# A Mamba stage in slots: the softplus logarithm in open PSUM sums, one activation table set for exp and log, seven of 32 state products per chunk on GpSimd, and VectorE's remaining product issued last in its slot

## The chip, the cores and the metric

The kernel runs on one core of one Trainium2 chip. The metric is device time in microseconds (us); a kernel is run several times and the median is compared. Engines are named as in the profile: PE is TensorE (PEld its weight loads), DVE is VectorE, ACT is ScalarE, POOL is GpSimd, SP is SyncE, which here only issues DMAs.

## The reference, cut to what matters

The whole network is a convolution with attention, then a two-direction Mamba layer with a small MLP, then a mixture of experts. The change touches the Mamba layer alone:

```python
dt = softplus(einsum('blr,dr->bld', dt, dt_proj_w) + dt_proj_b)
A = -exp(A_log)
dA = exp(dt[..., None] * A)
dBx = dt[..., None] * Bm[:, :, None, :] * xc[..., None]
def step(h, inp):
    dA_t, dBx_t, C_t = inp
    h = dA_t * h + dBx_t
    y = einsum('bds,bs->bd', h, C_t)
    return (h, y)
...
y = ys + xc * Dp
y = y * silu(z)
```

It is run over 4096 tokens, 512 inner channels and 16 states, once forwards and once backwards. The two results are added to `m`, and then come a layer norm, an MLP with a leaky ReLU, `m + p`, the residual, and a layer norm for the experts.

## The kernel before, in words

Everything is fp32. The Mamba layer is cut into 16 **chunks** of 512 tokens; even chunks are the forward direction, odd ones the backward direction. A chunk is cut into 32 **slots**, `at` = 0 to 31. A slot is (e, k, j): e = at // 8 is one of four tiles of 128 channels, k one of four groups of states, j one of two halves. So a slot is a [128, 2, 512] tile: 1024 elements in each partition. The order of all engines' queues is written out by hand in the loop over `slots` at the end of `mamba_phase`; nothing is reordered.

Each slot n needs, in this order:

- `inflow(n)` on POOL: dbx = dt·x · B, read from two tiles that DMAs have spread over the partitions. Three buffers, `up`.
- `decay(n)` on ACT: two exponentials of 512 elements into a PSUM tile `da`, of which there are two.
- `bring(n)` on ACT, or on POOL in the slots of `LONG`: one column of dbx gets the state that the chunk starts with.
- `recur(n)` on DVE: the scan h = da·h + dbx. Right behind it the product of h with C, into an SBUF tile `h` of which there are four (`hp`). In the slots of `POOLED` (4, 10, 12, 18, 28 before) the scan writes straight into `h`, and POOL makes the product in place (`pooled`), issued a slot later, behind `inflow`.
- `keep(n)` on ACT: a copy of the last column into `state`, issued a slot later, ahead of `decay(n + 2)`.
- `sum_states` on PE: four matmuls that add the states of a pair of slots into `y`, issued two slots after the pair's first, three where that one is pooled.
- `close(i, e)` on DVE, once in eight slots: y times the gate silu(z). Before the change it is issued in slots 0, 8, 16 and 24, behind the product.

In slot n the loop issues `inflow(n + 2)`, `keep(n - 1)`, `decay(n + 1)`, `bring(n + 1)` and `recur(n)`. The other work of the stage is spread among the slots as generators, one step a slot:

- `prepare(q)` makes chunk q's inputs while chunk q-1 is running. It starts in slot 27 of the chunk before that one (`AHEAD` = 5), and takes one step per slot: input projection, causal convolution on PE, SiLU of xc in slot 8, the x_proj matmul in slot 9, dt_proj in slots 11 to 14, then softplus, in the form relu(v) + log(1 + exp(-|v|)) with a rounding correction, the gate's projection z, and the products dt·x (`dt_piece`), which go through DRAM (`dtd`) to be spread over partitions.
- `output(i)` multiplies a finished chunk by the output weights, in slots 1 to 3 of the next one.
- `tail(c)` is the layer norm, MLP, residual and second layer norm for a pair of chunks. Each `yield` names the engine that its next step needs, and the step is taken only in slots that are not in `FULL` for that engine.

PSUM is small: two banks for `mm` (the projections, dt and softplus sums), one `tl` bank for the tail, one `y` bank, two `da` tiles. The SiLU of the gates runs in slot 0 (L2019), the one of xc in the step behind the convolution (L1389). The compiler puts an activation table load ahead of any activation whose function the loaded set lacks.

Of the kernel before, what the change touches and what calls it, by code (L numbers as in the profile page):

```python
# [1255 lines left out]
def mamba_phase(cx, early, w_in, w_x, w_out, w1, w2, x1d, ud, bcd, dtd, x2d, u2d, usum):  # L1256
# [12 lines left out]
    with ExitStack() as ctx:  # L1269
# [59 lines left out]

        def mm_psum():  # L1330
            return pmm.tile([P, N], FP, name="mm", tag="mm")
# [25 lines left out]
        def prepare(q):  # L1357
# [31 lines left out]
            nc.scalar.activation(xc, xc, AF.Silu)  # L1389
            yield  # L1390
            ps = mm_psum()
            nx = DR + 2 * DS
            for e in range(ET):
                nc.tensor.matmul(ps[0:nx, :], wx[d][:, e, :], xc[:, e, :], start=e == 0, stop=e == ET - 1)
            yield
            xd = few()[0:nx, :]
            nc.scalar.copy(xd, ps[0:nx, :])

# [7 lines left out]
            for e in range(ET + 1):  # L1406
                if e > 0:
                    ex = early.wide("ex")[:, :, 0:N] if e == 1 else ex
                    dt = dt or sp.tile([P, ET, N], FP, name="dt", tag="dt")
# [10 lines left out]
            for e in range(ET + 2):  # L1420
                if e < ET:
                    rd = rds[e] = few()
                    nc.scalar.activation(rd, ex[:, e, :], AF.Identity, scale=-1.0, bias=-1.0)
                    nc.scalar.add(rd, rd, 1.0)
                if e > 1:
                    nc.scalar.copy(dt[:, e - 2, :], sums.pop(e - 2))
                if 0 < e <= ET:
                    ps = sums[e - 1] = mm_psum()
                    for v, x in enumerate((rds.pop(e - 1), ex[:, e - 1, :], dt[:, e - 1, :])):
                        nc.tensor.matmul(ps, cx.ident, x, start=v == 0, stop=v == 2)  # L1430
                yield


            nc.scalar.activation(ex, ex, AF.Ln, bias=1.0)
            zs = in_pair(q, ET)
            yield
            got["dt"] = dt
            for at, (v, e) in enumerate(((0, 0), (1, 0), (0, 1), (0, 2), (0, 3), (1, 1))):
                if at == 3 and q > 1:
                    load_first(q, 0)  # L1440
                dt_piece(q, v, e, ex)
                if at in (0, 2):
                    z = sp.tile([P, 2, N], FP, name="z", tag="z", bufs=3)
                    got.setdefault("z", []).append(z)
                if at < 4:
                    nc.scalar.copy(z[:, at % 2, :], zs[at % 2])  # L1446
                if at == 1:
                    zs = in_pair(q, ET + 2)
                    if q + 1 < 2 * NCH:
                        load_u(q + 1)  # L1450
                yield

        def dt_piece(q, v, e, ex=None, eng=nc.gpsimd):
# [3 lines left out]
            if v == 0:  # L1457
                eng.tensor_tensor(dt[:, e, :], dt[:, e, :], ex[:, e, :], ALU.add)
                if q < 2:
                    return  # L1460
                if e == 0:
                    firsts[q] = ip.tile([P, ET], FP, name="first", tag="first", bufs=1)
                nc.gpsimd.tensor_tensor(firsts[q][:, e : e + 1], dt[:, e, 0:1], odd[:, 0:1], ALU.add)
                if e % 2:
                    first_rows[q, e // 2] = cx.rows.tile([P, 2], FP, name="first_row", tag="first_row", bufs=2)
                    nc.sync.dma_start(out=first_rows[q, e // 2], in_=firsts[q][:, e - 1 : e + 1])
# [70 lines left out]
        def tail(c):  # L1537
# [3 lines left out]
            yield from layer_norm(cx, tl, tl_psum, m, hn, nc.gpsimd, 2)  # L1541
            x1 = tl.tile([P, CT, N], FP, name="x1", tag="ln_xc")
            nc.sync.dma_start(out=x1, in_=x1d[c])
            for t in range(CT):
# [3 lines left out]
            yield "DMA"  # L1548
            yield "POOL"
# [34 lines left out]
        def start():  # L1584
# [93 lines left out]
            for z in got["z"]:  # L1678
                nc.scalar.activation(z, z, AF.Silu)
# [293 lines left out]
        with tc.manual_schedule(engines=ORDERED):  # L1973
# [5 lines left out]
            for n, (i, e, k, j) in enumerate(slots):  # L1979
# [40 lines left out]
                if i == 0:  # L2020
                    step(begin)
# [377 lines left out]
```

## Time and profile before

| | |
|---|---|
| median of 3 runs | 4099.89 us (4095.22 to 4108.44) |
| profiled execution, its own time | 4114.01 us |
| its span, first to last instruction | 4112.1 us |
| Mamba slots, first scan to last | 1946.9 to 3818 us of the span |
| time from a chunk's first scan to the next one's, chunks 4 to 14 | 113.5 to 119.2 us, mean 117 |
| one scan, 128x1024 | 2347 ns |
| one product with C on DVE, 128x1024 | 1225 ns |
| the same product on POOL | 2355 ns |
| one decay activation, 128x512 (two in a slot) | 692 ns |
| one ACT table load | 1283 ns |
| from scan to scan: slot with a DVE product / pooled slot | 3.59 us / 2.26 us |

The profile page gives busy time by engine and by line for one execution. Engine idle time has a releaser beside it: the instruction whose end let the engine go on. A fp32 matmul of 512 columns appears as two instructions; their pitch, not the modelled duration, tells how long PE is held: 0.43 us each where the granted clock is 1.0, 0.85 where it is 0.5.

### The profile page before, as it was taken

The numbers are of one execution on the slowest core, as the hardware profiler recorded it, in microseconds if no ns is written. First come the engines' busy times: TensorE is split into PE (matmuls) and PEld (weight loads), VectorE is DVE, ScalarE is ACT, GpSimd is POOL, SyncE is SP. The second block draws the span as 40 slices with busy tenths as digits, with TensorE's granted clock in tenths as the row PEclk, the third lists the DMA queues.
The fourth block names the chain that finished last, engine by engine and source line by source line (L and its number), as shares of the span: only waits on it lengthen the run. The fifth ranks groups of instructions, "written<-read, shape, count | busy, mean of one in ns | idle before, by whom it ended". The sixth has DMA issues, their size and how long they took to land. (4 is left out here: it accounts for less than half of the span.)

```text
span 4112.1 us, 43244 instructions
## 1 busy us (share of the span) xinstructions
PE 3586.2 (87%) x14792; PEld 1183.0 (29%) x14792; DVE 3503.9 (85%) x2919; ACT 2667.8 (65%) x4152; POOL 1836.6 (45%) x1284
## 2 busy tenths in 40 slices
PE   6769888999999999998888788888888888876898
PEld 2324332222222222222222222222223232222444
DVE  8998877989889889877899999999999999999322
ACT  1111226988887878876777777778787777775222
POOL 3020000000000000001888889888888989888100
PEclk9889998999999999998888998898899899888999
DMA  6232215223322223214334344344333434332221
GB/s 208 93 98 95 81 59 157 51 60 65 65 56 62 63 54 65 58 42 122 118 106 129 116 124 130 121 119 129 113 113 119 144 109 133 117 122 90 64 62 55
DMA packets 164324, 399.93 MB, mean 97 GB/s; under 512 B 36997, under 2 KB 46469, under 8 KB 163838
## 3 DMA queue, kind: packets, MB, share of 16 engines
q1 hardware_dynamic: 137166, 304.26, 24.0%
q0 software_dynamic: 24624, 84.43, 8.9%
q10 hardware_dynamic: 2304, 8.39, 0.6%
q8 instruction: 118, 1.93, 0.2%
q14 instruction: 112, 0.92, 0.1%
HBM read 268.17 MB, written 79.56 MB: 85 GB/s over the span
## 5 line engine op out<-in xcount | busy, mean ns | idle before, releaser
L1890 POOL TENSOR_TENSOR dbx<-dtxr,b 128x1024 f32<-128x1024 f32 x512 | 1202.9, 2360 | 201.9 <-DVE da L1903 80.2
L1044 ACT ACTIVATE e<-sc 128x1024 f32<-128x1024 f32 x1024 | 993.8, 1023 | 178.5 <-PE sc L1037 152.7
L1903 DVE TENSOR_TENSOR_SCAN da<-da,state,dbx 128x1024 f32<-128x1024 f32 x432 | 1013.9, 2347 | 16.9 <-ACT da L1880 7.2
L954 DVE TENSOR_TENSOR s<-s,e 128x1024 f32<-128x1024 f32 x768 | 880.5, 1216 | 25.1 <-ACT e L1044 24.4
L1880 ACT ACTIVATE da<-dtr,aneg 128x512 f32<-128x512 f32 x1024 | 708.2, 692 | 33.2 <-DMA dtr<-dtd 3.7
L1037 PE MATMUL sc<-q,kS 32*128 32x512 f32 x4096 | 652.8, 650 | 15.6 <-ACT e L1044 11.4
L961 PE MATMUL av<-e,vT 128*32 128x512 f32 x4096 | 557.2, 612 | 0.4 <-ACT e L1044 0.4
L1908 DVE TENSOR_TENSOR h<-da,c 128x1024 f32<-128x1024 f32 x432 | 529.1, 1225 | 33.2 <-PE y L1943 1.2
L977 POOL DMA_DIRECT2D s<-s x94 | 81.5, 874 | 953.0 <-DVE s L954 901.7
L1943 PE MATMUL y<-h,sel 128*32 128x512 f32 x2048 | 368.9, 654 | 99.2 <-DVE h L1908 74.7
L462 PE MATMUL cv<-v,u 128*128 128x512 f32 x928 | 414.9, 607 | 28.7 <-DVE v L286 13.3
L1037 PEld LDWEIGHTS sc<-q,kS 32*128 32x128 f32 x4096 | 211.5, 185 | 460.0 <-issue 259.4
L1339 PE MATMUL mm<-u,win 128*128 128x512 f32 x464 | 252.8, 695 | 77.1 <-ACT z L1446 25.8
L462 PEld LDWEIGHTS cv<-v,u 128*128 128x128 f32 x928 | 179.4, 195 | 261.9 <-issue 228.4
L560 DVE SCALAR_TENSOR_TENSOR acc<-pad,wdw_s,acc 128x768 f32<-128x768 f32 (+1 forms) x192 | 236.0, 1234 | 19.9 <-ACT acc L553 14.2
L1934 ACT COPY state<-da 128x2 f32<-128x2 f32 x431 | 67.9, 158 | 264.6 <-DVE h L1908 263.5
L1385 PE MATMUL mm<-xp,taps 128*128 128x512 f32 x480 | 212.8, 595 | 0.0
L143 POOL TENSOR_TENSOR ln_few<-ln_few,minus_half 128x4 f32<-128x4 f32 x29 | 34.8, 1201 | 397.5 <-DMA ln_few<-ln_row 259.6
L954 DVE TENSOR_TENSOR s<-e 128x1024 f32<-128x1024 f32 x128 | 151.9, 1217 | 62.2 <-ACT e L1044 53.5
L1903 DVE TENSOR_TENSOR_SCAN h<-da,state,dbx 128x1024 f32<-128x1024 f32 x80 | 187.5, 2344 | 13.0 <-ACT state L1934 11.7
L961 PEld LDWEIGHTS av<-e,vT 128*32 128x32 f32 x4096 | 82.0, 108 | 400.5 <-issue 390.3
L1913 POOL TENSOR_TENSOR h<-h,c 128x1024 f32<-128x1024 f32 x80 | 188.4, 2355 | 1.0 <-ACT state L1934 1.0
(379 smaller groups left out, 3940.9 us busy)
## 6 DMA issues: line engine op xcount, KB each, us to landing
dtr<-dtd SPq DMA_DIRECT2D x128, 512.0 KB
dtxr<-dtd SPq DMA_DIRECT2D x128, 512.0 KB
s<-s POOLq DMA_DIRECT2D x94, 512.0 KB, 5.9
b<-bcd SPq DMA_DIRECT2D x64, 256.0 KB
c<-bcd SPq DMA_DIRECT2D x64, 256.0 KB
dtd<-dt SPq DMA_DIRECT2D x64, 256.0 KB
dtd<-few SPq DMA_DIRECT2D x64, 256.0 KB
u<-uv SPq DMA_DIRECT2D x24, 640.0 KB
```

The lines of the kernel that those rows point to most:

```text
L462: nc.tensor.matmul(rows4(ps), u[:, dy, P * ci : P * ci + P], v[:, dy : dy + HR, ci, :], start=dy + ci == 0, stop=dy == k - 1 and ci == CT - 1,
L560: nc.vector.scalar_tensor_tensor(o, src, w_ap, o, ALU.mult, ALU.add)
L954: nc.vector.tensor_tensor(z, x, y, ALU.add)
L961: nc.tensor.matmul(g.av[32 * h : 32 * h + 32, :], vT[:, kb, P * t + 32 * h : P * t + 32 * h + 32], es[h // 2][:, h % 2, :], start=kb == 0, ...
L1037: nc.tensor.matmul(ps[h // 2][:, h % 2, :], kS[r, t, P * kb : P * kb + P], q_t[r, t, :], start=True, stop=True,)
L1044: nc.scalar.activation(e, ps[i], AF.Exp)
L1339: nc.tensor.matmul(ps, win[d][:, t, P * e : P * e + P], u[:, t, ::-1] if d else u[:, t, :], start=t == 0, stop=t == CT - 1,)
L1880: nc.scalar.activation(da[:, v, :], dts[i, e, j][0][:, v, :], AF.Exp, scale=aneg[i % 2][:, a : a + 1])
L1890: nc.gpsimd.tensor_tensor(u, dts[i, e, j][1], bcs[i, k][0][:, None, :].to_broadcast([P, 2, N]), ALU.mult)
L1903: nc.vector.tensor_tensor_scan(das[n].rearrange("p v n -> p (v n)"), da.rearrange("p v n -> p (v n)"), u.rearrange("p v n -> p (v n)"), st ...
L1908: nc.vector.tensor_tensor(h, da, bcs[i, k][1][:, None, :].to_broadcast([P, 2, N]), ALU.mult)
L1943: nc.tensor.matmul(ys[i, e][32 * j : 32 * j + 32, :], cx.sel, hs[n + j // 2][:, j % 2, :], start=False, stop=k == SQ - 1,)
```

## The change

1. `exp_and_log()` loads a table set that holds both exp and log, right behind each SiLU. Before, exp, log and SiLU were in three sets.
2. In `prepare`, log(1 + exp(-|v|)) is no longer added to dt on POOL. PE's sum of the other terms stays open (`stop=False`), ACT takes the logarithm by tiles of 512 (`logs`), and one more identity matmul adds it and closes the sum; ACT then copies the finished dt out (`keep_dt`). The first column, which the next chunk's start needs, is copied by ACT from PSUM, where POOL made it before.
3. The gate projections (`z_of`, `keep_z`) are spread: the first two beside x_proj (slots 9 to 11), the other two among the softplus steps. The dt·x pieces, four on POOL, are issued in slots 21, 23, 25 and 27, where before they ran from slot 29 on and into slot 4 of the chunk itself.
4. `POOLED` has seven slots in place of five.
5. `readout(n)`, DVE's product with C, is split off from `recur` and issued at the very end of a slot, behind `close`, the tail's and the output's DVE work. `close` is issued in slots 1, 9, 17 and 25.
6. In `tail`, m + x1 is made by PE (two identity matmuls for each half) and ACT copies in steps that only waited before; POOL's addition and two steps go. `FULL` is set anew, and the last chunk's double steps are taken out.

```diff
+        def exp_and_log():
+            nc.scalar.preload_act_table_set("natural_log_exp_and_others")
...
             nc.scalar.activation(xc, xc, AF.Silu)
+            exp_and_log()
...
+            z_of(q, 0)
             yield
             xd = few()[0:nx, :]
             nc.scalar.copy(xd, ps[0:nx, :])
+            keep_z(q, 0)
+            z_of(q, 1)
...
+            def total(e):
+                sums[e] = mm_psum()
+                for v, x in enumerate((rds.pop(e), ex[:, e, :], dt[:, e, :])):
+                    nc.tensor.matmul(sums[e], cx.ident, x, start=v == 0, stop=False)
+
+            def logs(e):
+                nc.scalar.activation(ex[:, e, :], ex[:, e, :], AF.Ln, bias=1.0)
+
+            def keep_dt(e):
+                nc.scalar.copy(dt[:, e, :], sums[e])
...
+            rounding(0)
+            yield
+            for e in range(ET + 1):
+                if e > 0:
+                    keep_dt(e - 1)
                 if e < ET:
+                    total(e)
+                if e < ET - 1:
+                    rounding(e + 1)
+                if 0 < e < 3:
+                    keep_z(q, e + 1)
                 yield
-            nc.scalar.activation(ex, ex, AF.Ln, bias=1.0)
-            zs = in_pair(q, ET)
...
+                if e < ET:
+                    logs(e)
+                    if e < 2:
+                        z_of(q, e + 2)
+                    nc.tensor.matmul(sums[e], cx.ident, ex[:, e, :], start=False, stop=True)
+                if e > 0:
+                    dt_piece(q, 1, e - 1)
...
-            nc.gpsimd.tensor_tensor(m, x1, m, ALU.add)
+                    nc.tensor.matmul(ps, cx.ident, m[:, waits - 1, :], start=True, stop=False)
+                    nc.tensor.matmul(ps, cx.ident, x1[:, waits - 1, :], start=False, stop=True)
...
+        def readout(n):
+            i, e, k, j = slots[n]
             if n % SPS not in POOLED:
-                nc.vector.tensor_tensor(h, da, bcs[i, k][1][:, None, :].to_broadcast([P, 2, N]), ALU.mult)
+                nc.vector.tensor_tensor(hs[n], das[n], bcs[i, k][1][:, None, :].to_broadcast([P, 2, N]), ALU.mult)
...
-        POOLED = {4, 10, 12, 18, 28}
+        POOLED = {0, 4, 8, 12, 16, 20, 28}
...
-            "PE": {0, 1, 2, 3, 4, 5, 6, 7, 9, 18, 19, 20, 21, 23, 24, 25, 27, 29},
-            "ACT": {0, 6, 7, 8, 9, 16, 17, 18, 19, 20, 21, 22, 23, 30, 31},
-            "POOL": {0, 1, 2, 4, 24, 25, 26, 27, 28, 29, 30, 31},
+            "PE": {1, 2, 3, 4, 5, 6, 7, 9, 18, 20, 21, 22, 24, 27, 29},
+            "ACT": {0, 6, 7, 8, 9, 14, 15, 16, 20, 22, 30, 31},
+            "POOL": {1, 5, 9, 13, 17, 21, 23, 25, 27, 29, 30, 31},
...
-                    if k == 0:
-                        close(*slots[n - 2][:2])
-                        if e == 0:
-                            out = output(i - 1)
+                if j == 2 and k == 0 and n > 2:
+                    close(*slots[n - 3][:2])
+                    if e == 0:
+                        out = output(i - 1)
...
+                readout(n)
             ending()
```

## The prediction

> **What bounds the kernel now.** I read the page's engine shares first, then windows, then VectorE's waits and timeline. The chain that ended last reaches back over only 8% of the span, so it says nothing of the Mamba slots. The window of chunks 4 to 14:
>
> ```profile
> core 0: us, PE busy (x) PEld busy (x) DVE busy (x) ACT busy (x) POOL busy (x), PEclk, DMA share, GB/s
> 2411.00:3697.00 1286.00, 1085.33 (x3052) 356.09 (x3048) 1235.63 (x753) 1004.76 (x1947) 1131.38 (x699) 0.89 0.40 122
> ```
>
> DVE is busy 96% of it, POOL 88%, PE 84% at a clock of 0.89, ACT 78%. DVE bounds the stage, but three others are close behind, with few buffers between. The costs:
>
> ```profile
> L1890 POOL TENSOR_TENSOR dbx<-dtxr,b 128x1024 f32<-128x1024 f32 x512 | 1202.9, 2360 | 201.9 <-DVE da L1903 80.2
> ...
> L1903 DVE TENSOR_TENSOR_SCAN da<-da,state,dbx 128x1024 f32<-128x1024 f32 x432 | 1013.9, 2347 | 16.9 <-ACT da L1880 7.2
> ...
> L1908 DVE TENSOR_TENSOR h<-da,c 128x1024 f32<-128x1024 f32 x432 | 529.1, 1225 | 33.2 <-PE y L1943 1.2
> ```
>
> On DVE's timeline a slot takes 3.59 us from scan to scan, a pooled one 2.26. What little DVE waits for, from chunk 1 on:
>
> ```profile
> DVE xc L1952 <- PE y L1943: 11.8, 7, 2.1
> DVE h L1903 <- ACT state L1934: 11.7, 13, 1.6
> DVE da L1903 <- POOL dbx L1926: 5.2, 4, 1.9
> ```
>
> The first is `close` in slot 16 of odd chunks, the second pooled scans in slots 10 and 12, the third slot 1. All gaps over 0.2 us in chunks 2 to 15 add up to 37.5 us, 2.7 a chunk.
>
> **Where ACT is the limit already.** Slot 0 of chunk 8, ACT's timeline:
>
> ```profile
> 2874.62 1.42 ACT L1880 ACTIVATE da<-dtr,aneg 128x512 f32<-128x512 f32 x2
> 2876.05 1.28 ACT L2019 ACT_TABLE_LOAD   x1
> 2877.34 2.00 ACT L2019 ACTIVATE z<-z 128x1024 f32<-128x1024 f32 x2
> 2879.25 0.14 ACT L1934 COPY state<-da 128x2 f32<-128x2 f32 x1
> 2879.41 1.28 ACT L1880 ACT_TABLE_LOAD   x1
> 2880.71 1.42 ACT L1880 ACTIVATE da<-dtr,aneg 128x512 f32<-128x512 f32 x2
> 2882.06 0.28 ACT L1928 ACTIVATE dbx<-dbx,brought 128x1 f32<-128x1 f32 x1
> ```
>
> DVE's scans start at 2874.30 (slot 0) and at 2882.37 (slot 2), 0.03 us behind the last of these rows. So from slot 0 to slot 2 ACT's chain takes 8.07 us, and DVE's own work 7.78.
>
> **The change part by part**, per chunk.
>
> *Two products leave DVE*: 2 x (3.59 - 2.26) = 2.7 us gained. POOL gets 2 x 2.36 and loses four dt additions (4 x 1.18), four first columns (4 x 0.19) and half of the tail's addition (2.35 / 2): 102.9 us a chunk before, 101.0 after, 87% of 116. What hides it is POOL's lead: dbx(n+2) may start once scan(n-1) is done, which leaves 6 us. The tightest stretch is slots 16 to 23 of even chunks: eight inflows, two products, two dt pieces, the tail's product, 28.8 us in DVE's 28.9. Without the lead each late us is DVE's; I take 0.
>
> The Trainium skill speaks against this part: "GPSIMD Engine Reference", section 1, says that GpSimd's SBUF interfaces are shared with VectorE and contend when a VectorE instruction has two SBUF inputs. The start of the stage shows it: the same addition on DVE took 0.69 us alone and 2.72 under POOL's first inflows.
>
> ```profile
> 1937.23 0.69 DVE L1622 SCALAR_TENSOR_TENSOR few<-few,ex 128x512 f32<-128x512 f32 x1
> ...
> 1939.68 2.72 DVE L1622 SCALAR_TENSOR_TENSOR few<-few,ex 128x512 f32<-128x512 f32 x1
> ```
>
> By the rule a slot's DVE work would stretch; by the rows it does not, since scan and product read `da` from PSUM and last 2347 and 1225 ns with POOL 88% busy.
>
> *`close` a slot later*: the wait in slot 16 goes, 11.8 / 14 = 0.8 us. In slot 17 the y sum has a pooled and a whole scan more. *Slots 10 and 12 no longer both pooled*: the waits there (13.5 us in 14 chunks) go, 1.0. *dt pieces earlier*: the slot 1 wait goes, 0.4.
>
> *`readout` behind other work*: a product starts 0.10 us after its scan has ended, an independent instruction 0.08 before (a tail operation at 2862.22 behind a scan that ended at 2862.30). In the seven slots a chunk where something now stands between, 0.15 each: 1.0. Queued behind a late `close` or tail operation is now `readout`, and for that wait `keep`, `decay` two slots on and PE's sum.
>
> Gains: 2.7 + 0.8 + 1.0 + 0.4 + 1.0 = 5.9 us a chunk.
>
> *Joint set*: six loads a chunk become four, ACT -2 x 1.28; four logarithms of 0.63 (the start's rows) for one of 1.92, +0.6; four one-column copies, between 0.16 and 0.19 by `keep`'s rows, +0.7; the tail's two copies 2 x 0.56 / 2. ACT -0.7. None of these loads stands where DVE waits (log ran in slot 23, unpooled), so 0 on the path. The skill ("ScalarE: Activation LUTs", "What ACT_TABLE_LOAD costs") adds a drain of 1380 ns to a load's 1283; in the rows above SiLU starts 0.01 us behind its load. By the page ACT would save 2.7 us more.
>
> *PE*: four identity matmuls, 4 x 0.86 (two instructions, 0.43 pitch), and the tail's four in two chunks: +5.2 us, 98.7 to 104 busy of 116.
>
> **What is late next.** (a) Slots 0 to 2: the 8.07 us chain is the same after, since the set is loaded behind SiLU at once. DVE's work there falls to 2.26 + 2.27 + 0.60 + 1.14 = 6.27, so the pooled slot 0 and the gap buy nothing: 1.5 given back. (b) Slots 8 to 10, the SiLU of xc with two loads: in chunk 8 ACT needs 7.95 us from scan(8) to decay and `bring` of 10; before DVE took 8.3, after it would take 7: 1.2 given back. (c) Slots 16 to 24: with 20 pooled, slot 20's ACT list (keep, decay, bring 1.95; dt and first column 0.75; rounding 1.24; z 0.56; then keep, decay, bring 1.8) lasts 6.3 us against 2.26 + 3.59; even chunks add the tail's 1.5 us affine in slot 21: 0.5 in odd, 1.7 in even chunks: 1.1. (d) Slots 8 to 12 of odd chunks. Going through the yields, the tail's first down-projection falls in slot 8, the second in slot 10. From scan(8) = 0: the tail's DVE operation ends at 3.0, four matmuls of 0.86 take down to 6.5, x_proj (8 x 0.43) 9.9, the two new z projections 11.7 and 13.4, second down 16.9, then skip and sum of slots 8 and 9, 18.9. Scan(12) is pooled and writes the buffer that this sum reads; DVE is there at 15.6. 3.3 us, 1.65 a chunk. In the same stretch `keep_z` on ACT waits for PE until 11.7; behind it stand keep(10), decay(12), `bring`, done at 14.2, in time.
>
> Given back: 1.5 + 1.2 + 1.1 + 1.65 = 5.45. Net 0.45 a chunk, 6 us in chunks 2 to 15. Besides: in the start two loads (rows of 1.28) go on the way to the first scan, 1.3 to 2.6, I take 2; chunk 0's close wait of 2.54 in slot 8 goes, and 1 of its ACT waits; chunk 1, without tail and bring, 1; in chunk 15 no `prepare` runs, so only (a) is given back, 4 more. Sum: 6 + 2 + 2.5 + 1 + 1 + 4 = 17 us. DMAs: the dt stores on SP now stand in slots 21 to 27, ahead of the loads of B and C in 24 to 30; those are first used in slot 30, some 20 us of cover; if POOL were two slots late 7 of it would be gone. The first columns' DMAs wait for ACT in place of POOL, five slots ahead of their use: 0.
>
> The profiled execution goes from 4114 to 4097. It is 14 us above the median of the runs, so for the median 4099.9 - 17 = **4083 us**.
>
> **Rivals.** *B, the cover holds*: (c) and (d) don't come, because a stall in slot 2 or 10 lets PE and ACT catch up. Net 3.2 a chunk: 14 x 3.2 + 10.5 = 55, so 4045. For it: PE's 98.7 us at a clock of 0.89 are 88 at full clock, 93 with the additions, of 116. Against: its timeline has no gap from slot 2 to slot 7, so it has nothing to catch up with there.
>
> *C, slower: PE's clock.* PE's clock halves after idle stretches:
>
> ```profile
> 2908.55 3.78 PE L1569 MATMUL tl<-a1a,w2s 128*128 128x512 f32 x4 [3.79 <-DVE m L1574]
> 2912.12 3.18 PE L1569 MATMUL tl<-a1b,w2s 128*128 128x512 f32 x4
> ```
>
> Here PE sat 3.79 us and the down-projection took 6.7 us instead of 3.4 (granted clock 0.50 to 0.55). In (d) I have PE idle 1.9 us ahead of it; at 3.5 or more it starts at half clock, and the same sum stops scan(12) for 3.4 us more per spell of 6.83 us, two at most: 20 to 41 us in six odd chunks. In slots 16 and 17 the new order leaves PE some 4.6 us idle, so the first open sum (2.6 us) runs at half clock and the sum that pooled scan(20) needs is up to 2.1 us late: up to 29 us in 14 chunks. It decides from 17 us on. One spell and half the second: 20 + 17 - 17, so 4120; all of it 4153. *D, the set is not shared*: eight more loads a chunk, 10.3 us on ACT in slots 19 to 25, of which some 4 are hidden: 16 x 6, so 4200; the load rows would show it.
>
> **How the numbers follow.** 0.3%, 12 us, is about what a measurement of this kernel tells from no change. Forecast 0.40 (4060 to 4100), B 0.30, C 0.28, D 0.02. Faster: B and 0.24 of the forecast, 0.54; same: 0.16 of it and 0.03 of C, 0.19; slower 0.27. The range takes in B's 4045 and most of C: 4042 to 4130.
>
> **What would show it.** From slot 0 to 2 still 8.07 us with DVE idle 1.8; slot 16's wait gone; four loads a chunk; scan(12) in odd chunks waiting for PE y; DVE waiting for ACT in slots 22 to 24; `dbx` hardly waited for. I am wrong if scan(2) starts before 8 us, or POOL appears as what DVE waits for, or PE's mean clock in the stage falls under 0.85.

## The result and the profile after

The kernel became slower by about a quarter of a per cent: 4115.3 us median (4108.35 to 4124.57) against 4104.9 (4092.3 to 4117.61) for the kernel before on the same chip, 20 runs each. The ratio is 1.0026, 95% interval [1.0017, 1.0035]. The forecast had been a gain of 0.4%.

The profiled execution of the changed kernel lasted 4108.35 us, which is less than the 4114.01 of the one before. That is no contradiction. Up to the last activation of the attention, where the code is the same, these two executions differ by 14.8 us (1880.0 and 1894.8 us; the kernels of the experiments, with the same code up to there, had 1883.8 to 1900.7). So the two are compared from there on:

| stretch, us | before | after | difference | forecast |
|---|---|---|---|---|
| last attention activation to first scan | 52.1 | 50.3 | -1.8 | -2 |
| chunk 0 | 119.9 | 125.6 | +5.7 | -3.5 |
| chunk 1 | 110.5 | 112.8 | +2.3 | -1 |
| chunks 2 to 14 | 1520.5 | 1532.8 | +12.3 | -6 |
| chunk 15 | 120.2 | 113.4 | -6.8 | -4 |
| behind the last scan | 294.1 | 291.6 | -2.5 | 0 |

That makes +9.2 us, which agrees with the medians' +10.4.

First the same window as before the change, chunks 4 to 14, from the view of windows:

```profile
core 0: us, PE busy (x) PEld busy (x) DVE busy (x) ACT busy (x) POOL busy (x), PEclk, DMA share, GB/s
2411.00:3697.00 1286.00, 1081.13 (x3176) 369.20 (x3177) 1195.98 (x729) 984.09 (x2009) 1108.40 (x624) 0.93 0.40 120
```

VectorE is busy 40 us less (1235.6 before) in a window of the same length: its share fell from 96% to 93%. Yet chunks 4 to 14 took 1298.0 us, 1286.7 before. The work did leave VectorE, and stalls took its place. PE's granted clock rose from 0.89 to 0.93, so PE isn't slower on the whole (one stretch of slots, shown below, is another matter). The costliest groups of the page, with busy time and mean duration, then idle time ahead and its main releaser:

```profile
L1941 DVE TENSOR_TENSOR_SCAN da<-da,state,dbx 128x1024 f32<-128x1024 f32 x400 | 938.9, 2347 | 58.5 <-ACT dbx L1971 17.4
...
L1951 DVE TENSOR_TENSOR h<-da,c 128x1024 f32<-128x1024 f32 x400 | 488.5, 1221 | 22.9 <-PE mm L1423 1.4
...
L1941 DVE TENSOR_TENSOR_SCAN h<-da,state,dbx 128x1024 f32<-128x1024 f32 x112 | 262.5, 2343 | 53.6 <-PE y L1986 44.1
L1956 POOL TENSOR_TENSOR h<-h,c 128x1024 f32<-128x1024 f32 x112 | 263.9, 2357 | 28.9 <-ACT state L1977 28.8
```

No instruction became dearer: the scan is at 2347 ns as before, VectorE's product at 1221 (1225), GpSimd's at 2357 (2355). What is new is the idle time ahead of the 112 pooled scans. VectorE's waits in the Mamba stage (in all, times, longest):

```profile
DVE h L1941 <- PE y L1986: 44.1, 24, 5.9
DVE da L1941 <- ACT dbx L1971: 17.4, 18, 1.8
DVE da L1941 <- ACT state L1977: 14.5, 14, 1.8
DVE da L1941 <- ACT da L1918: 14.2, 15, 3.6
DVE da L1941 <- POOL dbx L1969: 9.8, 6, 2.6
...
DVE usum L1617 <- POOL u L149: 6.3, 7, 1.7
```

Before, the longest rows of this kind were 15.5 and 11.7 us. Now pooled scans wait 44 us for PE's sum of an earlier pair, whose buffer they write, and some 46 us fall to the three kinds of wait for ScalarE.

All gaps of VectorE over 0.2 us in chunks 2 to 14 add up to 90.5 us, against 32.7 before: +57.8. The stretch grew by 12.3, so the other work gave 57.8 - 12.3 = 45.5 us, 3.5 a chunk.

One odd chunk shows the chain. This is PE's timeline in chunk 9, whose first scan starts at 2992.48:

```profile
2997.85 4.56 PE L1554 MATMUL mm<-xc,wout 128*128 128x512 f32 x10 [1.41 <-DVE xc L1995]
...
3019.33 2.52 PE L1986 MATMUL y<-h,sel 128*32 128x512 f32 x16
3023.69 1.98 PE L1605 MATMUL tl<-a1a,w2s 128*128 128x512 f32 x4 [1.85 <-DVE a1b L1600]
3025.51 1.88 PE L1605 MATMUL tl<-a1b,w2s 128*128 128x512 f32 x4
3027.32 3.63 PE L1398 MATMUL mm<-xc,wx 128*48 128x512 f32 x8
3030.89 3.70 PE L1342 MATMUL mm<-u,win 128*128 128x512 f32 x8
3034.43 1.88 PE L1605 MATMUL tl<-a1a,w2s 128*128 128x512 f32 x4
3036.14 1.88 PE L1605 MATMUL tl<-a1b,w2s 128*128 128x512 f32 x4
3037.86 1.02 PE L1984 MATMUL y<-xc,skip 128*128 128x512 f32 x2
3038.81 1.06 PE L1986 MATMUL y<-h,sel 128*32 128x512 f32 x8
```

and VectorE's row that waits for the last of these:

```profile
3039.98 2.35 DVE L1941 TENSOR_TENSOR_SCAN h<-da,state,dbx 128x1024 f32<-128x1024 f32 x1 [3.66 <-PE y L1986]
```

From the output projection in slot 1 on, PE has one gap of note, 1.85 us, in 41 us. Between the sum of slots 6 and 7 and the sum of slots 8 and 9 stand two down-projections, x_proj and two gate projections (3030.89). Scan(12) writes the buffer that the second sum reads.

A second chain stands in slots 16 to 22. The same chunk, from PE's first open softplus sum to scan(22):

```profile
3060.85 2.08 PE L1438 MATMUL mm<-few,ident 128*128 128x512 f32 x2 [4.34 <-ACT few L1433]
...
3070.14 1.02 PE L1471 MATMUL mm<-ex,ident 128*128 128x512 f32 x2
```

```profile
3071.20 0.59 ACT L1444 COPY dt<-mm 128x512 f32<-128x512 f32 x1 [1.54 <-PE mm L1471]
```

```profile
3075.17 2.36 DVE L1941 TENSOR_TENSOR_SCAN da<-da,state,dbx 128x1024 f32<-128x1024 f32 x1 [0.75 <-ACT dbx L1971]
```

PE sat idle for 4.34 us, and between scan(16) and scan(20) its granted clock was 0.57. The sum that closes the first tile of dt came late, ScalarE stood 1.54 us for it, and with it the decay of slot 22.

### The profile page after: what moved, and what is told of

Same layout as the page of the kernel before. It is cut to its first block, busy times and chain, and to the rows that moved or that the text cites. A ratio compares the mean times of both kernels' runs of the same rounds, so it can differ in the third digit from the quotient of the medians.

```text
span 4106.5 us, 43589 instructions
## 1 busy us (share of the span) xinstructions
PE 3577.7 (87%) x14968; PEld 1200.4 (29%) x14968; DVE 3456.2 (84%) x2887; ACT 2640.9 (64%) x4233; POOL 1814.7 (44%) x1193
## 5 line engine op out<-in xcount | busy, mean ns | idle before, releaser
L1941 DVE TENSOR_TENSOR_SCAN da<-da,state,dbx 128x1024 f32<-128x1024 f32 x400 | 938.9, 2347 | 58.5 <-ACT dbx L1971 17.4
L1951 DVE TENSOR_TENSOR h<-da,c 128x1024 f32<-128x1024 f32 x400 | 488.5, 1221 | 22.9 <-PE mm L1423 1.4
L1986 PE MATMUL y<-h,sel 128*32 128x512 f32 x2048 | 335.8, 629 | 95.0 <-DVE h L1951 77.2
L1941 DVE TENSOR_TENSOR_SCAN h<-da,state,dbx 128x1024 f32<-128x1024 f32 x112 | 262.5, 2343 | 53.6 <-PE y L1986 44.1
L1956 POOL TENSOR_TENSOR h<-h,c 128x1024 f32<-128x1024 f32 x112 | 263.9, 2357 | 28.9 <-ACT state L1977 28.8
L1342 PE MATMUL mm<-u,win 128*128 128x512 f32 x464 | 237.7, 654 | 30.7 <-ACT xp L1370 28.1
L954 DVE TENSOR_TENSOR s<-e 128x1024 f32<-128x1024 f32 x128 | 152.0, 1217 | 59.2 <-ACT e L1044 50.3
L961 PEld LDWEIGHTS av<-e,vT 128*32 128x32 f32 x4096 | 81.7, 108 | 394.4 <-issue 386.7
```

The source lines that it names most:

```text
L954: nc.vector.tensor_tensor(z, x, y, ALU.add)
L961: nc.tensor.matmul(g.av[32 * h : 32 * h + 32, :], vT[:, kb, P * t + 32 * h : P * t + 32 * h + 32], es[h // 2][:, h % 2, :], start=kb == 0, ...
L1941: nc.vector.tensor_tensor_scan(das[n].rearrange("p v n -> p (v n)"), da.rearrange("p v n -> p (v n)"), u.rearrange("p v n -> p (v n)"), st ...
L1951: nc.vector.tensor_tensor(hs[n], das[n], bcs[i, k][1][:, None, :].to_broadcast([P, 2, N]), ALU.mult)
L1956: nc.gpsimd.tensor_tensor(hs[n], hs[n], bcs[i, k][1][:, None, :].to_broadcast([P, 2, N]), ALU.mult)
L1986: nc.tensor.matmul(ys[i, e][32 * j : 32 * j + 32, :], cx.sel, hs[n + j // 2][:, j % 2, :], start=False, stop=k == SQ - 1,)
```

## The experiments

The labels e1 to e18 are the names that the expectations use. Ratios are to the kernel before, timed on the same chip. Stalls are VectorE's gaps over 0.2 us in chunks 2 to 14 of the profiled run. There is one such execution for each kernel, and its length can differ from what the ratio says: in e1 the time from the attention to the end is 11.5 us shorter than in the kernel before, and the medians are equal. So the stalls tell where VectorE waits; what an edit is worth is told by the ratio.

### The parts alone

**The late order alone** (e4): the kernel before, with `readout` last in its slot and `close` a slot later.

```diff
+                if j == 2 and k == 0 and n > 2:
+                    close(*slots[n - 3][:2])
...
+                readout(n)
```

> The kernel before with one part of the change alone: the product with C issued at the end of its slot, and the gate (close) a slot later. Theory 1: the gate's waits of slots 8 and 16 go (10.5 us in chunks 2 to 14, 2.5 in chunk 0), and the gap behind the scan in some seven slots a chunk, 0.84 x 15 = 13 us; with nothing given back 25 us faster than before, 0.994. Rival (a later product holds the PSUM tile longer, so ACT's decay comes late): no gain, 1.000, with DVE waiting for ACT behind slots 1, 9, 17 and 25.

Measured 0.9998 [0.9986, 1.0009], as the rival said. The waits of slot 16 for PE went (10.5 us before), but stalls are 40.0 against 32.7: VectorE now waits for ScalarE, in odd chunks 7.2 us in slot 10 and 4.2 in slot 25. A wait removed on one engine uncovered the next. That is not the whole account: in the profiled execution chunks 2 to 14 took 1508.8 us against 1520.5, and what follows the last scan 5.5 us more; why the medians show no gain stays open.

**The joint set alone** (e7): `exp_and_log()` behind each SiLU, nothing else.

```diff
             nc.scalar.activation(xc, xc, AF.Silu)
+            exp_and_log()
```

> The kernel before with the joint table set alone; the logarithm stays one activation in slot 23. Theory 1 (no load stood where DVE waits, but for the start): the start gets 2 us shorter, nothing else, 0.9995. Rival (ACT's two loads a chunk count): 14 us faster or more, 0.9965.

Measured 0.9983 [0.9972, 0.9995], stalls 24.6. The waits of slot 1 for `dbx` (5.2 us) went, and slot 16's fell from 10.5 to 6.3. I had costed the set at 2 us in the start and nothing on the path; it is worth 0.17%, 7 us (by the interval 2 to 11), and the stalls of VectorE that shrank are those behind GpSimd and PE. Theory and rival both missed.

**Seven pooled slots alone** (e8).

```diff
-        POOLED = {4, 10, 12, 18, 28}
+        POOLED = {0, 4, 8, 12, 16, 20, 28}
```

> The kernel before with the seven pooled slots alone. Theory 1 (slots 0, 8 and 16 hold ACT's SiLU chains or a gate that waits for PE, so a shorter DVE slot there turns into a wait): of 2.66 us a chunk nearly all is given back, 0.998 to 1.002, with slot 16's close waiting 1.3 us longer. Rival (each product moved is 1.33 us): 43 us faster, 0.9896.

Measured 1.0051 [1.0030, 1.0071], stalls 81.7. VectorE's waits in that kernel:

```profile
DVE xc L1952 <- PE y L1943: 28.8, 9, 4.6
DVE da L1903 <- ACT state L1934: 21.7, 20, 2.2
```

The two products that leave VectorE are worth 2 x 1.33 x 13 = 35 us in these chunks; the stalls grew by 49. Alone, the step that was to bring the most loses, more than either expectation allowed.

**Late order and joint set together, with five pooled slots** (e12): the two diffs above in one kernel.

> The kernel before with two parts of the change, the joint set and the late product with the late gate. Theory 1 (they save in different places: the set in slots 1, 16 and the start, the late order the gap behind the scan): 0.9975 or less, better than either alone. Rival (the late order's gain is taken back by ACT's chains, as alone): 0.9983 as the set alone.

Measured 0.9961 [0.9948, 0.9974]: 0.4% faster than before, without the seven slots and without the softplus part. The three parts alone multiply to 0.9998 x 0.9983 x 1.0051 = 1.0032, but parts do not simply multiply: these two would give 0.9981. That the product comes near the 1.0026 of the whole change, which has the softplus part besides, is chance.

**The change with the old tail** (e15; its old steps and its old `FULL`; the double steps of the last chunk back):

```diff
+            nc.gpsimd.tensor_tensor(m, x1, m, ALU.add)
...
+                for _ in range(1 + (i == 2 * NCH - 1 and at in (4, 6, 7))):
```

> The changed kernel with the tail part undone: m + x1 on POOL, the old FULL table and the last chunk's double steps. Theory 1 (the tail's new places, both down-projections in slots 8 and 10 of odd chunks, are what fills PE's chain there): scan(12)'s 24 us of waiting in odd chunks go, but the tail's up- and down-projections meet x_proj and the new z projections in other chunks, as in the kernel before; 5 to 15 us faster than the changed kernel, 0.999 to 1.0015. Rival (the softplus and z part alone costs it): 1.0026 or more.

Measured 1.0042 [1.0023, 1.0061], stalls 83.0. The theory, a gain over the change, missed: the new tail doesn't cost the loss. The interval overlaps the change's own, so that it helps isn't shown.

### PE's queue in odd chunks

**The tail kept out of slot 10** (e1), so that the second down-projection leaves the chain ahead of scan(12):

```diff
-            "PE": {1, 2, 3, 4, 5, 6, 7, 9, 18, 20, 21, 22, 24, 27, 29},
+            "PE": {1, 2, 3, 4, 5, 6, 7, 9, 10, 18, 20, 21, 22, 24, 27, 29},
```

> The changed kernel with slot 10 closed to the tail's PE steps, so that in odd chunks the second down-projection is issued in slot 11, behind the sum of slots 8 and 9, and the steps after it a slot later. Theory 1 (the lost time is a buffer chain: pooled scan(12) waits for the sum of slot 8, which stands on PE behind that down-projection): the waits of 3.66 us and more in slot 12 of odd chunks go, 24.2 us in all, some of it comes back at the next limit; 20 us faster than the changed kernel, about 0.9975 of the kernel before. Rival 1 (POOL with seven products is the limit): no change, 1.0026, and the wait moves to POOL. Rival 2 (PE as a whole is too slow): the wait comes back in slots 13 to 20, 1.001 or more.

Measured 1.0000 [0.9986, 1.0013]. Scan(12)'s wait in odd chunks fell from 24.2 to 2.4 us in six chunks, as named. Some came back: 4.0 us in slot 14, where the layer norm waits for the moved PE work, and 8.2 instead of 2.9 in slot 16 of even chunks. Slots 20 to 24 stall 8.9 us instead of 16.2.

**The first two gate projections in slots 16 and 17** (e5), out of the same chain from its other end:

```diff
-            z_of(q, 0)
             yield
...
-            keep_z(q, 0)
-            z_of(q, 1)
...
             nc.scalar.activation(ex, ex, AF.Exp, scale=-1.0)
+            z_of(q, 0)
...
             rounding(0)
+            keep_z(q, 0)
+            z_of(q, 1)
```

> The changed kernel with the first two gate projections (z of tiles 0 and 1) moved from slots 9 and 10 to slots 16 and 17, where PE is idle for 4.3 us. Theory 1 (in odd chunks PE's unbroken chain from the gate's close in slot 1 to the sum of slot 8 is what bounds slots 1 to 12): the two projections, 2 x 1.75 us, leave the chain, scan(12)'s wait falls from 3.66 us to about 0.2 in each of six odd chunks, PE's half-clock spell in slots 16 to 18 gets shorter; 20 us faster than the changed kernel, about 0.9975. Rival (POOL or ACT is the limit in those slots, PE's wait only stands in front): no change, 1.0026, with ACT or POOL named in slot 12 instead of PE.

Measured 0.9981 [0.9966, 0.9995]. Scan(12)'s wait went from 24.2 to 6.4 us; slot 16 in even chunks now waits 14.0 us for PE. For scan(12) both experiments say the same: the wait is queue length on PE ahead of one sum. This one does a second thing. The projections fill PE's idle time in slots 16 and 17, the granted clock between scan(16) and scan(20) rises from 0.57 to 0.86 in chunk 9 and from 0.75 or more to 0.99 or more in even chunks, and the stalls of slots 20 to 24 fall from 16.2 to 2.4 us. How the gain splits between the two isn't shown.

**Slot 0 not pooled** (e2). This tells whether the pooled slot 0, which gains VectorE nothing while ScalarE's chain sets slot 2, can be dropped for free.

```diff
-        POOLED = {0, 4, 8, 12, 16, 20, 28}
+        POOLED = {4, 8, 12, 16, 20, 28}
```

> The changed kernel with slot 0 taken out of POOLED (six products on POOL). Theory 1 (ACT's chain of 8.07 us sets slots 0 to 2, so the pooled product there bought nothing and exposed the dbx of slot 1): slots 0 and 1 together stay at 8.1 us in odd chunks and fall from 8.5 to 8.1 in even ones, where POOL's dbx was waited for; 2 to 6 us faster than the changed kernel, more with chunk 0, about 1.001. Rival (each product moved saves DVE 1.33 us): 16 x 1.33 = 21 us slower, 1.0078.

Measured 1.0087 [1.0068, 1.0107]: a clear miss of the theory that slot 0 is idle ballast. Two rows of PE in its chunk 9, which starts at 3002.46:

```profile
3009.03 1.12 PE L1554 MATMUL mm<-xc,wout 128*128 128x512 f32 x2 [2.60 <-DVE xc L1995]
...
3053.12 1.06 PE L1986 MATMUL y<-h,sel 128*32 128x512 f32 x8
```

The output projection goes on 6.57 us after the chunk's start (5.37 in the changed kernel, from the rows above), because the scan and the product of slot 0 stand ahead of `close`. PE sat 2.60 us in place of 1.41 and then ran at a granted clock of 0.66 for 5 us (3009 to 3014; 1.00 in the changed kernel's 2997 to 3002). Its sum of slots 8 and 9 starts 50.7 us after the chunk's start, against 46.3. A gap of 2.29 us ahead of the first down-projection and a second stretch at half clock (3037.6 to 3041.1) follow. The rival's 1.0078 lies inside the interval, but not for its reason: slots 0 and 1 together took 8.22 us in odd chunks against 8.11, as the theory said, and scan(8) and scan(12) of these chunks wait 45.7 us for PE against 24.2. So a pooled slot 0 buys PE's start, not VectorE's time.

**Slots 0 and 8 not pooled** (e3).

```diff
+        POOLED = {4, 12, 16, 20, 28}
```

> The changed kernel with slots 0 and 8 taken out of POOLED: five products on POOL as before the change, in slots 4, 12, 16, 20 and 28. Theory 1: the sum of slots 8 and 9 is issued in slot 10, ahead of the down-projection, so scan(12) no longer waits for it (24 us in 13 chunks), scan(8) no longer for the sum of slot 4 (7 us), slot 1 hardly for dbx (10 us); slots 8 and 9 grow by the 1.3 us less what ACT's chain had given back, 0.5 a chunk. 30 us faster than the changed kernel, 0.995. Rival (products moved are what counts): 2 x 16 x 1.33 = 43 us slower, 1.013.

Measured 1.0062 [1.0046, 1.0078], between theory and rival, a miss too. Scan(12) no longer waits, but the layer norm in slot 13 of odd chunks waits 15.0 us for PE. The chain is PE's; without the pooled scan the next reader of PE meets it.

### Do seven slots pay inside the change?

**The change with the old five slots** (e9), and **the same with the gate projections moved as above** (e10):

```diff
+        POOLED = {4, 10, 12, 18, 28}
```

> The changed kernel with the old five pooled slots (4, 10, 12, 18, 28) and all else of the change. Theory 1 (the seven slots give nothing net, and what costs is PE's chain in odd chunks, on which the new z projections and both down-projections stand): PE's chain stays, so DVE waits for PE around slots 12 and 13 of odd chunks as in e3; 1.002 to 1.006. Rival (the seven pooled slots alone are what makes the change lose, as 1.0051 for them alone would have it): 0.9975 to 0.999, like the joint set alone.

> e5 (z projections in slots 16 and 17) with the old five pooled slots. Theory 1: the waits of pooled scans that stand four slots apart go (slot 8: 7 us, 12: 6, 16: 14, in 13 chunks) and those of slots 1 and 2 shrink by some 15, against 2.66 x 13 = 35 us more work on DVE: 0.996 to 0.999, no worse than e5's 0.9981. Rival (seven pooled slots do pay once PE's chain is short): 1.004 or more.

Measured 1.0061 [1.0045, 1.0077] and 1.0029 [1.0015, 1.0043]. Against 1.0026 and 0.9981 with seven slots: in the change the seven at their new places gain 0.35% on the five at their old ones, and 0.48% with the shorter chain. The first is inside its theory's range, but the theory's ground, that the seven give nothing, is not; the second missed its theory (0.996 to 0.999). With the five, VectorE's longest wait is

```profile
DVE da L1941 <- ACT dbx L1971: 32.6, 29, 1.7
```

of which 22.1 us are in slot 19, behind the pooled slot 18, where the new ScalarE steps (rounding, copies of dt and z) now stand. The places of the pooled slots belong to the order of the other engines, and the old places don't suit the new order (that these steps cause it is read from the order of the code, not tried).

The first of these runs also prices the part that no run has alone. It is the late order and the joint set (e12, 0.9961 on the same chip, with the same five slots) with the softplus part, the spread gate projections and the new tail added: 1.0061. The added parts cost 1.0%, some 41 us, more than the whole change loses. Among VectorE's stalls are those 22.1 us of slot 19, and 13.4 us behind PE in slots 12 and 13 of odd chunks, where e12 has none behind PE. The late order and the joint set with seven slots and without the softplus part were not run, so whether the seven pay there stays open.

**Seven slots at other places** (e11), with the gate projections moved:

```diff
+        POOLED = {2, 4, 10, 12, 18, 26, 28}
```

> e5 with seven other pooled slots, 2, 4, 10, 12, 18, 26 and 28: no two of them four slots apart, so no pooled scan writes the buffer of another pooled slot's sum, and none in slots 0, 8 and 16. Theory 1 (the distance of four, with its sum issued one slot ahead, is what turns the gain into waits for PE): the waits for PE y of scans in slots 8, 12 and 16 (27 us in e5) go, 0.993 to 0.996. Rival (POOL cannot make two products in three slots, or ACT cannot keep up): DVE waits for POOL's dbx or ACT's decay behind slots 4, 12 and 28, 0.999 or more.

Measured 1.0043 [1.0030, 1.0056], a miss. Waits for PE's sums went, and two others came:

```profile
DVE da L1941 <- ACT dbx L1971: 35.4, 23, 2.8
DVE usum L1617 <- POOL u L149: 29.5, 7, 4.9
```

Slot 19 waits 22 us for ScalarE as with the old five, and the tail's sums in slot 29 wait 25 us for GpSimd, which has the products of slots 26 and 28 in its queue.

### The chunk's start and the first chunk

In the changed kernel GpSimd's second inflow of chunk 10, the scan behind it, and the two issues on SP's queue whose loads these two slots read:

```profile
3115.55 2.35 POOL L1928 TENSOR_TENSOR dbx<-dtxr,b 128x1024 f32<-128x1024 f32 x1 [2.95 <-DMA dtxr<-dtd]
```

```profile
3118.21 2.36 DVE L1941 TENSOR_TENSOR_SCAN da<-da,state,dbx 128x1024 f32<-128x1024 f32 x1 [2.33 <-POOL dbx L1969]
```

```profile
3104.10 0.51 SPq L1539 DMA_DIRECT2D dtr<-dtd  x1
3107.13 0.51 SPq L1539 DMA_DIRECT2D dtxr<-dtd  x1
```

The load of dtxr is issued 3.03 us behind the load of dtr, and lands at 3115.40, 1.26 us behind it and 1.86 us behind the chunk's first scan (3113.54). In chunks 2 to 14 it lands between 1.25 us ahead of the first scan and 2.11 behind; VectorE stalls in slot 1 in the six chunks where it lands 0.33 behind or later, and in none where it lands 0.38 ahead or earlier. In the kernel before, a landing up to 1.54 us behind the first scan did no harm, and the loads came no sooner (1.75 ahead to 3.37 behind). What changed is the distance to scan(1): a free slot 0 lasted 4.18 us with its product and `close`, and lasts 2.26 now. In chunks 2 to 14 there are six such waits in slot 1, and in each of these six chunks scan(8) then waits for PE's sum (7.1 us in all), and in no other: `close` stands behind the stalled scan in slot 1, and PE's chain starts when `close` ends.

**dtxr loaded ahead of dtr, alone** (e18):

```diff
-            for v, nm in enumerate(("dtr", "dtxr")):
+            for v, nm in ((1, "dtxr"), (0, "dtr")):
```

> The changed kernel with one edit: the load of dtxr issued ahead of the load of dtr. Theory: GpSimd's first product of a chunk starts about 1.7 us sooner (the distance of the two issues on SP's queue), the waits of the scan in slot 1 for GpSimd's dbx (9.8 us in chunks 2 to 14) go below 2 us, and the kernel stands at 0.999 to 1.0010 of the time before instead of 1.0026. Rival: ScalarE's chain in slots 0 to 2 ends last anyway, so that the stall only moves to slot 2 and the ratio stays at 1.0020 to 1.0030.

Measured 1.0005 [0.9992, 1.0019], loop 1873.1 us instead of 1884.6. Waits of slot 1 for GpSimd: none above 0.2 us; the load of dtxr now lands 0.69 to 3.89 us ahead of the first scan. (The 1.7 us of the expectation are the distance of a later pair of loads, issued at 3111.16 and 3112.83.) The rival is right about VectorE in these slots: 1 and 2 together stall 25.6 us against 25.0, now for ScalarE, nearly all in slot 2.

```profile
DVE h L1941 <- PE y L1986: 33.0, 17, 3.7
```

The gain, as far as the stalls show it, comes from later in the chunk: with `close` on time, the waits in slot 8 (7.1 us) are gone, and those of the tail's sums in slot 29 (5.3 us), while slots 10 and 16 stall 7.9 us more.

**The gate projections moved and the tail out of slots 10 and 14** (e13), then **the same with dtxr loaded first** (e14):

```diff
+            "PE": {1, 2, 3, 4, 5, 6, 7, 9, 10, 14, 18, 20, 21, 22, 24, 27, 29},
```

> e5 (z projections in slots 16 and 17) and the tail's PE steps also kept out of slots 10 and 14, so that neither the second down-projection nor the sum with the residual stands ahead of the y sums of slots 8 and 12. Theory 1 (the waits of pooled scans for PE in slots 12 and 16 are each a y sum behind tail work on PE): e5's 6.4 us in slot 12 of odd and 14 us in slot 16 of even chunks go; 16 us faster than e5, 0.994 to 0.9955. Rival (PE is simply full; work moved away from one sum stands ahead of the next): 0.9975 or more, with the waits in slots 13 to 20.

> e13 with the two loads of a block swapped on SP: the tile for dbx first, the one for decay behind it. Theory 1 (scan(1)'s wait for dbx in even chunks, 12.9 us in e5, is the landing of that load, which is issued 1.7 us behind the other and lands 2.7 us later, with 2.35 us of POOL after it): the wait shrinks by 1 to 1.7 us in each of some six chunks, 8 us faster than e13. Rival (what the decay tile loses is lost on ACT): no faster than e13, DVE waiting for ACT in slots 1, 9, 17 or 25 instead.

Measured 0.9956 [0.9940, 0.9972] and 0.9926 [0.9905, 0.9947]; the second takes 4079.8 us and beats both kernels. The two intervals overlap, so what the order of the loads adds here isn't shown. Its longest waits:

```profile
DVE da L1941 <- ACT state L1977: 28.7, 22, 2.2
DVE da L1941 <- ACT da L1918: 24.6, 25, 3.6
```

No wait for PE's sum is left among the large ones; the largest are those for ScalarE.

**The first chunk with its old five slots**, in the changed kernel (e6), then added to the better version without (e16) and with the new order of loads (e17):

```diff
+        FIRST = {4, 10, 12, 18, 28}
+        def on_pool(n):
+            return n % SPS in (POOLED if n >= SPS else FIRST)
```

> The changed kernel, but the first chunk keeps the old five pooled slots (4, 10, 12, 18, 28). Theory 1 (chunk 0 lost 5.7 us because its own dt pieces are on POOL as well, and a pooled product in slot 0 delays the dbx of slots 4 and 5 by 3.7 us): chunk 0 takes 120 to 121 us instead of 125.6, 5 us faster than the changed kernel, 1.0013. Rival (the joint set and the moved steps are what slows chunk 0): it stays at 125.

> e13 with the old five pooled slots in the first chunk. Theory 1: chunk 0 falls from 124 or 125 us to 120 as in e6, and the total by 4 us against e13. Rival (as e6's total seemed to say, what chunk 0 saves comes back in chunk 1's loads): equal to e13.

> The change with z0 and z1 projected in slots 16 and 17, the tail's last steps kept out of slots 10 and 14, dtxr loaded ahead of dtr, and the old five pooled slots in the first chunk alone. If the first chunk's lengthening is time that the kernel pays (theory), it saves the 4 us that the first chunk gave in the run that had it without the new order of loads (124.3 to 120.2 us): 0.9926 - 0.0010 = 0.9916 of the time before, loop near 1838 us. If the second chunk takes it back (rival), it is equal to the run with the loads swapped, 0.9926, and chunk 1 is 3 to 4 us longer than there.

Measured 1.0027 [1.0010, 1.0044], 0.9933 [0.9912, 0.9953] and 0.9923 [0.9902, 0.9944]. In the first two, chunk 0 took 120.1 and 120.2 us instead of 125.6 and 124.3. In the third, chunk 0 itself took 126.2, but its first scan came 6.6 us sooner (42.9 us after the attention, 49.5 in the run with the loads swapped), so start and chunk 0 together took 169.1 against 174.3. Each saving of 4 to 6 us is under what the intervals tell apart. Whether the first chunk's loss is paid by the whole kernel stays open.

## Why the prediction was wrong

The direction was wrong: 17 us less were forecast, and 10.4 more were measured. (The forecast of 4083 us stands on a median of three runs, 4099.9; twenty gave 4104.9.) Per chunk, means over chunks 2 to 14:

| step of the prediction | forecast, us | measured, us |
|---|---|---|
| work that leaves VectorE or closes up (2.7 + 1.0) | 3.7 | 3.5 |
| (a) slots 0 to 2 | 1.5 | 1.9, of it 0.75 behind GpSimd in slot 1 |
| (b) slots 8 to 10, SiLU of xc | 1.2 | 0.5 |
| (c) slots 20 to 24, ScalarE's list | 1.1 | 1.2, of it 0.9 behind PE's late sums |
| (d) scan(12) of odd chunks behind PE's queue | 1.65 | 1.9 |
| stalls that no step names | 0 | 1.4 |

**The gains held.** The two products and the closed gap gave 3.5 of 3.7. GpSimd's longer list made neither scan nor product longer. The prediction read the rule of the Trainium skill ("GPSIMD Engine Reference", section 1) as a reason against this part. As quoted it names VectorE instructions with two SBUF inputs; scan and product have one each, beside `da` in PSUM, so the rule and the rows agree. The row that decides is VectorE's product: 1221 ns after, 1225 before.

**Mechanism (d) held, step by step.** In chunk 9 PE's gap ahead of the first down-projection is 1.85 us (1.9 forecast), the sum of slots 8 and 9 ends 19.2 us after scan(8) (18.9), and scan(12) waits 4.0 us on average in the odd chunks (3.3). (a) held where the load of dtxr was in time: slot 2 starts 8.1 us after slot 0 (8.07). Slot 16's wait went in odd chunks. The table loads are four a chunk.

**(c) came out right in size by luck.** The forecast let ScalarE's list in slot 20 last 6.3 us against VectorE's 5.85. In chunk 9 the work in that list takes 5.8 us, which fits; the 1.54 us of waiting for PE's sum make it too long. The chunks tell the two apart:

| chunks | PE's granted clock, scan(16) to scan(20) | ScalarE waits for the first tile's sum, us | VectorE's stalls in slots 20 to 24, us a chunk |
|---|---|---|---|
| 2, 6, 14 | 0.87 | 0 | 0 |
| 10 | 0.87 | 0.28 | 0.28 |
| 4, 8, 12 | 0.75 to 0.76 | 1.35 to 1.76 | 1.25 to 1.66 |
| odd | 0.56 to 0.60 | 0.75 to 1.63 | 1.47 to 2.27 |

The list is the same in all of them. (The 0.7 us of slot 24 in odd chunks also follow two short waits for PE, at full clock.) The forecast gave 1.7 us to even chunks, for the tail's affine, and 0.5 to odd ones; it came the other way round. The gate projections in slots 16 and 17 took the stalls of slots 20 and 22 away.

**The step that failed is the sum of what is given back**, "1.5 + 1.2 + 1.1 + 1.65 = 5.45": 7.0 were measured (90.5 / 13), with at most 0.3 of it left over from the 2.5 of before by the forecast's own steps. The four named steps came to 5.5 together; 1.4 stand in stalls that the sum leaves out, scan(8) in even chunks (6.6 us in 13 chunks), the tail's sums behind GpSimd in slot 29 (5.3), scan(16) in even chunks (2.9), and smaller ones. Two errors lie behind that:

- *"dt pieces earlier: the slot 1 wait goes"* looked at GpSimd's queue alone. The wait grew from 5.2 to 9.8 us: the load of dtxr comes no sooner, and scan(1) comes 1.9 us sooner, because slot 0 has neither product nor `close` any more. Swapping the loads removes it, and with it the wait in slot 8.
- Step (d) walked PE's queue from slot 8 in odd chunks, and not from the chunk's start in all of them. The chain begins with `close` in slot 1, so a delay ahead of that point comes out where a pooled scan needs a sum: 8, 12 or 16. The runs without the pooled slot 0 and with the loads swapped show this from both sides.

**The edges failed as well.** The forecast took 3.5 us off chunk 0, where 5.7 were added; chunk 1 was +2.3 instead of -1. Together they are 12.5 us off, against 18.3 in chunks 2 to 14; chunk 15 (-6.8) and the time behind the last scan gave 5.3 more than forecast. In chunk 0 scan(4) waits 2.7 us for GpSimd's `dbx`, where the cover of 6 us that the forecast gave GpSimd isn't there, and scan(8) 3.3 us for ScalarE's decay; with the old five slots in the first chunk it took 120.1 us. Why chunk 1 got longer stays open.

**"Joint set: 0 on the path"** was too low: alone the set is worth 0.17% [0.05, 0.28], whose low end is the 2 us that the forecast gave it in the start, but on top of the late order it brings the ratio from 0.9998 to 0.9961, some 15 us.

**The signs and the rivals.** One sign that the prediction named for being wrong came: GpSimd appears as what VectorE waits for, 9.8 us in slot 1 and 6.3 us at the tail's sums. B, the cover holds, asked for gains without (c) and (d); stalls came in both places. C, PE's half clock, had two halves. The first didn't come: the gap ahead of the down-projection is 1.85 us, the clock there 1.00, and scan(12) waits from queue length alone. The second, that the first open sum runs at half clock behind an idle stretch in slots 16 and 17, came and is what stands under (c), at 11.8 us in slots 20 and 22 where up to 29 were allowed. (C's middle case, "20 + 17 - 17", takes 17 for half of 29.) In chunks 2 to 14 as a whole the time at half clock fell from 332.5 to 211.6 us. D didn't happen. The case that came true, that the give-back outweighs the gain by a little, was inside the range but had no name.

## What to carry to other kernels

When work leaves the busiest engine, write each other engine's queue as a chain from the event that starts it, and set its end against the busiest engine's new, shorter time; a mean busy share says nothing of that, and neither does a mean clock. A load that is in time may be late when work ahead of its reader goes: the reader comes sooner. Price a stall twice: once where it stands, and once at the instruction queued behind it that starts another engine's chain. Time the parts of a joint change alone and in pairs: here one part lost alone, paid inside the whole, and paid more after the queue that it ran into was shortened.

## What the runs showed of the hardware

- PE's clock halved after gaps shorter than the 3.79 us of the prediction's rows: in the run without a pooled slot 0 after gaps of 0.90 and 2.60 us with 3.8 us of work between them (granted clock 0.66 from 3009 to 3014); after 0.90 and 1.41 us at the same place of the changed kernel it stayed at 1.00. In chunks 2 to 14 of the changed kernel 18 of 32 stretches at half clock begin with no gap above 2.6 us in the 7 us ahead of them. The Trainium skill ("TensorE: Matmul & The Clock Gate", Part 1) speaks of an idle window of about 3.4 us; no single gap in the places just named is that long, and a lower clock came all the same.
- Two loads that one loop issues side by side are not issued or landed together. For the pair that slot 1 reads, in chunks 2 to 14 of the changed kernel, the second is issued 0.60 to 3.03 us behind the first and lands 1.24 to 2.40 us behind it. With the order swapped, GpSimd's second product of chunk 10 starts 0.75 us ahead of the chunk's first scan instead of 2.01 behind it.
